# Twenty-two transfers move from SyncE's queue to GpSimd's in an attention and experts kernel

## The chip, the cores and the metric

The kernel runs on one core of a Trainium2 chip. The core has TensorE (PE), VectorE (DVE), ScalarE (ACT), GpSimd (POOL) and SyncE (SP). SP does no arithmetic here: it waits for semaphores and issues transfers. The metric is the device time of one execution in microseconds (us); lower is better. Times without another name are places in the one profiled execution, counted from its first instruction.

## The reference

A layer of cross attention is followed by a layer of nine experts, all in float32. `ctx` has 77 rows per batch, so each of 16 heads has 77 keys.

```python
# x (4, 1024, 256), ctx (4, 77, 256), fside (4, 16)
def xattn(x, latents, shift, scale, ...):
    xn = layernorm(x, ln1_w, ln1_b)          # x is ctx here
    ln = layernorm(latents, ln2_w, ln2_b)    # latents: the normalised input
    q = (ln @ Wq) * (1 + scale) + shift
    k, v = split(xn @ Wkv)
    attn = softmax(q @ k.T * DIM_HEAD ** -0.5)
    return (attn @ v) @ Wout
def ffn(x, Wr, Wg, Wu, Wd):
    probs = softmax(x @ Wr); two largest of nine, made to sum to one -> cw
    hidden = silu(x @ Wg[e]) * (x @ Wu[e])
    return sum over e of cw[e] * (hidden @ Wd[e])
x = x + xattn(ctx, norm(x), fside, fside, ...)
x = x + ffn(norm(x), ...)
```

## The kernel before

The 4096 tokens are cut into eight groups of 512 (`g`), and each group into four sub-blocks of 128 tokens. That makes 32 sub-blocks (`i`). After a preparation of the weights, the attention's loop runs over the sub-blocks. The experts follow: each takes blocks of 128 or 256 tokens that were routed to it.

**One turn of the attention's loop.** TensorE makes the scores of sub-block `i` (`scores`), ScalarE their exponentials (`exponentials`). VectorE makes the attention's weights of sub-block `i-1` in the tile `an` (`attention_weights`) and turns them in blocks of 32 into `anT`, of which there is one buffer. `weights_turn` has SyncE write `anT` to a scratch tensor in HBM (`a_d`, line 332) and, when that has landed, read it back in another order into `aT` (line 335, four transfers). Three sub-blocks later, `values` lets TensorE use `aT` as its stationary operand (`po`, line 344), and `attended` adds the product to the input in place, in the tile `x` of that group. Four buffers hold four groups' `x`.

**What is done once per group, at fixed turns of the loop.** For turn `i = 4g + s`:
- `load_x(g + 2)`, at `s = 1`: the input two groups ahead comes in, 512 KB, 4 KB in each of 128 partitions. Groups 0 and 1 are loaded ahead of the loop. Two turns later VectorE takes its statistics (`query_stats`, `bn_q`).
- `residual`, at `s = 3`, for group `g - 1`: the finished sum is written to the output (512 KB, line 861). The experts later add their part to the output there (`adding`, line 1378, indirect transfers on POOL).
- `places`, at `s = 3`, for group `g - 2`: eight indirect transfers on POOL write the group's entries into the experts' lists in HBM (`list_d`, line 965). Each moves 128 entries of 8 bytes.
- `normalised`, at `s = 0`, for group `g - 2`, counted from the turn it is in: ScalarE makes the experts' normalised input `y`, which is written to the scratch tensor `y_d` (512 KB, line 896). The experts gather their tokens from it (`inputs`, lines 1208 and 1225).
- `choices`, at `s = 1`: the routing. POOL makes three tiny tiles for it (lines 932 and 937).

**What sets the order.** The order on each engine is the order of the program's text. A transfer is issued when its engine's queue comes to it and its semaphores allow, and an instruction that waits holds everything behind it on that engine. On SyncE the order of one turn is: `a_d` of the last sub-block, the wait for it, its four `aT` reads, then what that turn has of the group's three transfers, then `a_d` of the next. From about 322 us on, the first experts' weights come in on SyncE too (lines 1191 to 1201).

Of the kernel before, what the change touches and what calls it, by code (L numbers as in the profile page):

```python
# [15 lines left out]
P = 128  # L16
# [5 lines left out]
def kernel(  # L22
# [18 lines left out]
    nc = tc.nc  # L41
# [11 lines left out]
    NS = TB // P  # L53
# [37 lines left out]
    x_v = x.flatten_outer_dims().rearrange("(g p s) d -> g p s d", p=P, s=NS)  # L91
    out_r = out.flatten_outer_dims()
    out_v = out_r.rearrange("(g p s) d -> g p s d", p=P, s=NS)
# [5 lines left out]
    y_d = dram.tile([TOK, D], F32, name="y_d")  # L99
# [102 lines left out]
    xg = {}  # L202

    def load_x(g):
        xg[g] = pools["xpool"].tile([P, NS, D], F32, tag="x", name=f"x{g}")
        nc.sync.dma_start(out=xg[g], in_=x_v[g])

    zscale, zstats = {}, {}

# [21 lines left out]
    def off_mean(name, g, mv, r):  # L231

        o = stat.tile([P, NS], F32, tag=name, name=f"{name}{g}")
        nc.vector.scalar_tensor_tensor(o, mv[:, :, 0], -1.0, r, ALU.mult, ALU.mult)
        return o
# [128 lines left out]
    with ExitStack() as kvs:  # L364
# [104 lines left out]
        for b in range(B):  # L469
# [12 lines left out]
            out=wrow, in_=ln2_w.rearrange("(o d) -> o d", o=1).to_broadcast([P, D])  # L482
# [105 lines left out]
        def router_weights():  # L588
# [26 lines left out]
            out=before, in_=ones, pattern=[[1, P]], compare_op=ALU.is_gt, fill=0.0, base=0,  # L615
# [64 lines left out]
        kvs.close()  # L680
        open_attention()
        load_x(0)
        load_x(1)
        for b in range(B):
            nc.vector.tensor_copy(g_sb[b][:, :, HJ:], wz)
            for t in range(2):
                for k in range(NP // QT):
                    nc.sync.dma_start(
                        out=g_sb[b][P - 1 : P, C - 1, :HJ].rearrange(
                            "p (q t k j) -> p q t k j", q=QT, t=2, j=J  # L690
                        )[:, :, t, k, :],
                        in_=brow.rearrange("(q r) k m -> q r k m", q=QT)[
                            :, t * B + b, k, b * J : (b + 1) * J
                        ],
# [163 lines left out]

    def residual(g):

        nc.sync.dma_start(out=out_v[g], in_=xg[g])
        mv = stat.tile([P, NS, 2], F32, tag="mvf", name=f"mv_f{g}", bufs=2)
        st = fstats.pop(g)
        for s in range(NS):
            yield nc.vector.bn_aggr(mv[:, s, :], st[:, s, :])
        routed[g] = dict(mv=mv)
# [19 lines left out]
    def normalised(g):  # L886

        y = pools["rpool"].tile([P, NS, D], F32, tag="y", name=f"y{g}", bufs=1)
        r = routed[g]["r"]
        o = off_mean("fo", g, routed[g]["mv"], r)  # L890
        for s in range(NS):
            yield nc.scalar.activation(
                y[:, s, :], xg[g][:, s, :], AF.Identity,
                bias=o[:, s : s + 1], scale=r[:, s : s + 1],
            )
        nc.sync.dma_start(out=y_d.rearrange("(g p s) d -> g p s d", p=P, s=NS)[g], in_=y)

    def choices(g):

# [540 lines left out]
    def routing(g):  # L1440

        yield from residual(g)
        root(g)
        yield from logits(g)
        exponential(g)
        yield from normalised(g)
        yield from choices(g)
        yield from listed(g)
# [9 lines left out]
    for i in range(N_SUB + 1):  # L1458
        g, s = divmod(i, NS)
        now_on = i < N_SUB  # L1460
        d = i - LAG
# [44 lines left out]
        if s == 1 and g + 2 < NG:  # L1506
            load_x(g + 2)
# [5 lines left out]
        if gr >= 0 and sr == 1:  # L1513
            if g + 2 < NG:
                query_variance(g + 2)
            if q >= 0:
                advance(residual(q))
                root(q)
            if g + 2 < NG:
                query_root(g + 2)  # L1520
            nc.scalar.activation(junk, eps_t, AF.Exp)
            if q > 0:
                advance(places(q - 1))
        if gr >= 0 and sr == 2 and q >= 0:
            advance(logits(q))
            exponential(q)
            advance(normalised(q))
# [125 lines left out]
```

## Time and profile before

| What | Value |
|---|---|
| median of 3 executions | 898.35 us (897.76 to 902.75) |
| the profiled execution's own time | 902.66 us |
| its span, first to last instruction | 900.6 us |
| TensorE busy in the span | 869.1 us, 97% |
| VectorE, ScalarE, GpSimd busy | 592.2, 356.2, 312.5 us |
| SyncE's transfers (q1 of the page) | 162.90 MB, 60.5% of 16 engines' time |
| GpSimd's transfers (q0) | 17.26 MB, 10.3% |
| granted TensorE clock, mean | 0.992 |

The profiled execution is one of its own: 902.66 us lies 4.31 us above the median. The span leaves 2.06 us of it outside. A row of waits says which instruction waited for what, for how long in total, how often, and at most. A row of the timeline has the start, the duration, the engine, the line, and in brackets the idle time of the engine just before it. In the windows, "DMA share" is the mean busy share of the core's 16 transfer engines, and GB/s is what they moved. [...]

### The profile page before, as it was taken

How to read it: one execution, taken by the hardware profiler on the slowest of the kernel's cores; microseconds unless marked ns; L12 is line 12 of the kernel's file. 1: busy time of each engine (PE TensorE's matmuls, PEld its weight loads, DVE VectorE, ACT ScalarE, POOL GpSimd, SP SyncE). 2: the span in 40 equal slices, each digit the busy share in tenths (PEclk: the TensorE clock that was granted, in tenths of full speed). 3: DMA queues.
4: the chain of work that ended last, by engine and by line, in shares of the span. 5: the costliest groups of instructions: out<-in, count | busy, mean ns of one | idle time of the engine just before them, and what ended most of it. 6: DMA issues, size and time to landing. Idle time of an engine off the chain costs nothing. (4 is left out here: it accounts for less than half of the span.)

```text
span 900.6 us, 13822 instructions
## 1 busy us (share of the span) xinstructions
PE 869.1 (97%) x3864; PEld 677.8 (75%) x3864; DVE 592.2 (66%) x1806; ACT 356.2 (40%) x1500; POOL 312.5 (35%) x325
## 2 busy tenths in 40 slices
PE   8999999998999998899999999999999999999996
PEld 6545787866787776788787777777777777778885
DVE  4857788778999978443826666666666656665641
ACT  3668687858788685241121111111111111111110
POOL 3000000404233430537256435435445435445232
PEclk9999999999999999899999999999999999999998
DMA  6116556566766676899579779779779778789722
GB/s 222 49 67 202 152 187 193 113 182 149 216 176 191 188 210 203 213 298 185 158 226 298 218 220 315 223 217 311 224 221 317 219 217 218 226 230 322 217 33 24
DMA packets 132956, 181.18 MB, mean 201 GB/s; under 512 B 26951, under 2 KB 98127, under 8 KB 132752
## 3 DMA queue, kind: packets, MB, share of 16 engines
q1 hardware_dynamic: 115322, 162.90, 60.5%
q0 software_dynamic: 17344, 17.26, 10.3%
q8 instruction: 31, 0.51, 0.3%
q14 instruction: 45, 0.37, 0.1%
q10 hardware_dynamic: 214, 0.13, 0.0%
HBM read 141.54 MB, written 40.39 MB: 202 GB/s over the span
## 5 line engine op out<-in xcount | busy, mean ns | idle before, releaser
L1265 PE MATMUL pg<-xT,wgu 128*128 128x256 f32 x1144 | 253.0, 380 | 3.0 <-DVEq L1606 1.5
L1265 PEld LDWEIGHTS pg<-xT,wgu 128*128 128x128 f32 x1144 | 215.5, 190 | 33.0 <-ACT xT L1254 2.5
L286 ACT ACTIVATE ex<-psc,mx 128x77 f32<-128x77 f32 x512 | 158.7, 331 | 70.3 <-DVE mx L275 66.6
L1343 PE MATMUL po<-wd,hid 128*128 128x256 f32 (+1 forms) x804 | 180.9, 380 | 0.0
L1343 PEld LDWEIGHTS po<-wd,hid 128*128 128x128 f32 (+1 forms) x804 | 149.2, 187 | 28.1 <-issue 3.7
L344 PE MATMUL po<-u,aT 128*128 128x265 f32 x640 | 159.2, 405 | 8.8 <-DMA aT<-a_d 8.8
L344 PEld LDWEIGHTS po<-u,aT 128*128 128x128 f32 x640 | 150.4, 313 | 11.6 <-issue 9.9
L1378 POOL DMA_INDIRECT out_dram<-co,ids x63 | 100.2, 1591 | 167.7 <-DVE co L1346 139.4
L965 POOL DMA_INDIRECT list_d<-r_entry,r_pli x64 | 66.8, 1043 | 260.9 <-DVE r_pli L963 148.1
L1238 DVE STREAM_TRANSPOSE xT<-yin 32x128 f32<-32x128 f32 (+1 forms) x544 | 148.4, 273 | 12.5 <-DMA yin<-y_d,ids 3.7
L271 PE MATMUL psc<-g,zT 128*128 128x462 f32 (+1 forms) x384 | 141.5, 514 | 2.6 <-ACT zT L260 2.6
L1271 ACT ACTIVATE sl<-pg 128x256 f32<-128x256 f32 x130 | 49.7, 384 | 233.8 <-PE pg L1265 162.1
L1272 DVE TENSOR_TENSOR hid<-pg,sl 128x256 f32<-128x256 f32 x130 | 55.0, 424 | 128.9 <-ACT sl L1271 94.7
L271 PEld LDWEIGHTS psc<-g,zT 128*128 128x128 f32 x384 | 71.7, 190 | 61.0 <-issue 46.0
L286 ACT ACTIVATION_READ_ACCUMULATOR ex<-psc,mx 128x1 f32 x512 | 107.9, 211 | 0.0
L327 DVE STREAM_TRANSPOSE anT<-an 128x1280 f32<-128x1280 f32 x32 | 79.6, 2486 | 14.3 <-DMA a_d<-anT 13.8
L1208 POOL DMA_INDIRECT yin<-y_d,ids x67 | 70.5, 1053 | 27.0 <-issue 25.5
L275 DVE TENSOR_REDUCE mx<-psc 128x6 f32<-128x462 f32 (+1 forms) x96 | 53.5, 558 | 18.8 <-PE psc L271 17.7
L1346 DVE TENSOR_SCALAR co<-po,ids 128x256 f32<-128x256 f32 x67 | 32.2, 483 | 48.4 <-PE po L1343 46.8
L308 DVE TENSOR_TENSOR an<-ex,rs 128x1024 f32<-128x1024 f32 x32 | 39.2, 1225 | 1.1
L1331 ACT COPY hid<-ph 128x384 f32<-128x384 f32 x15 | 7.2, 479 | 78.4 <-PE ph L1326 78.4
L1307 ACT ACTIVATE hs<-psg 128x512 f32<-128x512 f32 x15 | 9.0, 597 | 65.3 <-issue 42.2
(311 smaller groups left out, 762.5 us busy)
## 6 DMA issues: line engine op xcount, KB each, us to landing
wgu<-in_L_ffn_Wg_dram SPq DMA_DIRECT2D x41, 704.0 KB
wd<-in_L_ffn_Wd_dram SPq DMA_DIRECT2D x41, 640.0 KB
wgu<-in_L_ffn_Wu_dram SPq DMA_DIRECT2D x41, 512.0 KB
a_d<-anT SPq DMA_DIRECT2D x32, 640.0 KB
aT<-a_d SPq DMA_DIRECT2D x128, 160.0 KB
wgu<-in_L_ffn_Wu_dram SPq DMA_DIRECT2D x41, 128.0 KB
x<-in_x_dram SPq DMA_DIRECT2D x8, 512.0 KB
out_dram<-x SPq DMA_DIRECT2D x8, 512.0 KB
```

What stands on the lines that cost most here:

```text
L271: nc.tensor.matmul(psc[:, :w], zT[:, c, :], g_sb[i // NS // GPB][:, c, h * J : h * J + w], start=(c == 0), stop=(c == C - 1),)
L275: nc.vector.tensor_reduce(nmx[i][:, h : h + n], psc[:, : n * J].rearrange("p (h j) -> p h j", h=n), AX.X, ALU.max, negate=True,)
L286: nc.scalar.activation(exs[i][:, h + q, :], pscs[k][:, q * J : (q + 1) * J], AF.Exp, bias=nmx[i][:, h + q : h + q + 1], accum_out=sms[i][: ...
L327: nc.vector.transpose(turned.rearrange("p q t k -> p q k t"), an_of[0].rearrange("p (k q t) -> p q k t", q=NQ, t=Q))
L344: nc.tensor.matmul(po[:, :DE], aT[:, :, n], u_sb[b][:, n, :], start=(n == 0), stop=(n == KC - 1))
L965: i = nc.gpsimd.indirect_dma_start(out=list_d[:, :], out_offset=bass.IndirectOffsetOnAxis(ap=place_i[:, s : s + 1], axis=0), in_=entries[k ...
L1208: return nc.gpsimd.indirect_dma_start(out=dst, out_offset=None, in_=src, in_offset=bass.IndirectOffsetOnAxis(ap=offsets, axis=0), **kw,)
L1238: yield nc.vector.transpose(xT[q : q + Q].rearrange("p c (h t) -> p h c t", t=P)[:, :nh, :, a : a + Q], of(yins, j)[a : a + Q].rearrange(" ...
L1265: nc.tensor.matmul(pg[:, g, :], w[:, c, at : at + P], xT[:, c, :], start=(c == 0), stop=(c == C - 1),)
L1272: nc.vector.tensor_tensor(hid[:, f, :], pg[:, 1, :], sl, ALU.mult)
L1343: nc.tensor.matmul(po[rows, :D], hid[:, f, at], d[:, f, :], start=(f == 0), stop=(f == NF))
L1378: i = nc.gpsimd.indirect_dma_start(out=out_r, out_offset=bass.IndirectOffsetOnAxis(ap=rows_of(j, h, rows), axis=0), in_=cos[j][:, h, :], i ...
```

## The change

Three transfers of each group change the engine that issues them: the input from the third group on (6 transfers), the residual (8) and the experts' input (8). The computation, the tiles, the buffers and the place in the program's text are the same.

```diff
@@ load_x
-        nc.sync.dma_start(out=xg[g], in_=x_v[g])
+        (nc.sync if g < 2 else nc.gpsimd).dma_start(out=xg[g], in_=x_v[g])
@@ residual
-        nc.sync.dma_start(out=out_v[g], in_=xg[g])
+        nc.gpsimd.dma_start(out=out_v[g], in_=xg[g])
@@ normalised
-        nc.sync.dma_start(out=y_d.rearrange("(g p s) d -> g p s d", p=P, s=NS)[g], in_=y)
+        nc.gpsimd.dma_start(out=y_d.rearrange("(g p s) d -> g p s d", p=P, s=NS)[g], in_=y)
```

In the instruction lists of the two programs TensorE's, VectorE's and ScalarE's order is the same. SyncE's list loses the 22 transfers; the `a_d` writes and `aT` reads stay on it, beside the weights. On GpSimd's list they stand, for one group in the middle of the loop, as: residual of group `q`, the eight list entries of group `q-1`, experts' input of group `q`, input of group `q+4`, the three tiny tiles of the routing of `q`. The inputs of groups 2 and 3 stand at the head of this stretch, right behind the three clearing instructions (lines 198 and 200) that open the attention. The residual of the last group stands behind the eight list entries of group 6, with the last experts' input behind it, and then the first `adding`.

## The prediction, made before the changed kernel ran

> **What bounds the kernel.** The page's first part comes first: TensorE is busy 97% of the span, so a change can save only in its gaps, and can lose by making new ones. The moved transfers all lie between 34 and 404 us. I therefore asked who waits for whom, in the whole span (columns: total us, times, longest).
>
> ```profile
> PE po L344 <- DMA aT<-a_d: 8.8, 5, 3.6
> DVE anT L327 <- DMA a_d<-anT: 13.8, 7, 3.4
> SPq L335 <- DMA a_d<-anT: 144.7, 30, 9.9
> SPq L206 <- DVE num L639: 19.1, 1, 19.1
> DVE bn_q L213 <- DMA x<-in_x_dram: 2.1, 1, 2.1
> POOL list_d L965 <- DVE r_pli L963: 148.1, 3, 127.9
> ```
>
> The loop's own path to HBM and back is what reaches TensorE: `a_d` late stops VectorE (one `anT` buffer), `aT` late stops TensorE. SP's long waits are for `a_d` itself, not for the moved transfers. Next, SP's timeline shows what stands in front of a late `a_d`:
>
> ```profile
> 150.56 0.34 SPq L332 DMA_DIRECT2D a_d<-anT  x1
> 153.56 1.74 SPq L335 DMA_DIRECT2D aT<-a_d  x4
> ...
> 164.14 0.43 SPq L861 DMA_DIRECT2D out_dram<-x  x1
> 168.94 0.34 SPq L332 DMA_DIRECT2D a_d<-anT  x1
> 178.84 1.75 SPq L335 DMA_DIRECT2D aT<-a_d  x4
> 180.68 0.38 SPq L896 DMA_DIRECT2D y_d<-y  x1
> 181.37 0.34 SPq L332 DMA_DIRECT2D a_d<-anT  x1
> 189.43 1.74 SPq L335 DMA_DIRECT2D aT<-a_d  x4
> 191.22 0.43 SPq L206 DMA_DIRECT2D x<-in_x_dram  x1
> 191.99 0.34 SPq L332 DMA_DIRECT2D a_d<-anT  x1
> ```
>
> From `a_d` to its `aT` is its latency: 3.0 us with a free queue (150.56 to 153.56), 8.1 behind `y` (181.37 to 189.43), 7.9 behind `x` (191.99, its `aT` at 199.88), 9.9 behind the residual and beside eight list transfers (163.6 to 174.2). TensorE's timeline shows what arrives:
>
> ```profile
> 186.82 4.91 PE L344 MATMUL po<-u,aT 128*128 128x265 f32 x20 [2.08 <-DMA aT<-a_d]
> ...
> 207.97 0.44 PE L258 MATMUL pz<-ident,z 128*128 128x128 f32 x2 [2.38 <-ACT z L249]
> ...
> 358.69 6.56 PE L344 MATMUL po<-u,aT 128*128 128x265 f32 x20 [3.57 <-DMA aT<-a_d]
> ...
> 379.16 6.56 PE L344 MATMUL po<-u,aT 128*128 128x265 f32 x20 [2.31 <-DMA aT<-a_d]
> ```
>
> With gaps of 0.55, 0.21, 0.51 and 0.87 us (at 227, 232, 247, 308), the middle has 6.6 us of gaps, the end of the attention 6.2 with one of 0.32 at 350. The last two cost more than idle time: their twenty matmuls take 6.56 us instead of 4.86, because the granted clock is 0.50 at 360 to 362 and 0.54 at 382 to 384. Outside these, TensorE runs turn after turn of 9.1 us without a gap, and nothing can be won.
>
> **SP's sequencer.** It loses 14 issues of 0.43 and 8 of 0.38 us, 9.0 us in all. SP waits 144.7 us for `a_d` anyway: 0.
>
> **POOL's sequencer.** It gains 22 issues. The nearest rows are its two transfers with 128 rows, 0.57 and 0.56 us, with 0.30 us between issues: 22 x 0.87 = 19 us, in a stretch in which POOL is mostly idle (in 260 to 280 it does nothing). In order of the queue, the waits: a residual waits for VectorE's sum, done 10 us before the list entries behind it can start; `y` waits for ScalarE, which is done (172.9) before those entries (174.2); the input behind it needs the residual landed two turns earlier; the three tiny tiles then come at 176.5, and VectorE uses them at 193.7. Cost 0. Without that cover, list entries 2 us late would still be in time: the first gather of the lists is at 299.
>
> **The start.** Inputs 2 and 3 no longer wait for SP's turns (input 2 was issued at 75.0, input 3 at 110.0): they stand behind a memset at 34.7 to 35.0 and start beside inputs 0 and 1 (34.6). VectorE already waits 2.09 us there, until 38.41, and TensorE hangs on this by ScalarE's chain at 45.4. The windows show inputs 0 and 1 moving at 270 to 401 GB/s from 36 to 39. If POOL's data flows from 37 at an even share of 400, the 150 KB left of input 0 take 0.4 us longer. Input 1 lands near 41.3 instead of 39.8, and is wanted at 41.3. Bounds: 0, and 2.6 us (1 MB at 400 GB/s put fully in front). Taken **+0.4**.
>
> **The middle, what goes.** `a_d` no longer stands behind `y` and `x` in one queue. The gaps that hang on this are 2.38, 0.21, 0.51 and 0.87, 4.0 us. But the residual, free of SP's wait for `aT`, now goes when VectorE's sum is done (194.3 for group 2, before 208.4), which meets the `a_d` issued at 191.99. Bounds -4.0 and 0. The Trainium skill ("DMA: Bandwidth & Descriptors", section "Issuing engines are not separate DMA queues") says that transfers from several issuers run on the same 16 engines and interleave, so another issuer saves only issue time. By this rule the term is 0; by the row (8.1 and 7.9 against 3.0 us, for 512 KB that needs 1.3 us at 400 GB/s) it is -4.0. The row is about order rather than sharing, so I lean to it: **-2.5**. The residual is also gone from in front of the `a_d` at 168.94; its 9.9 us are mostly the list entries' (the window from 171 has a share of 1.67 at 58 GB/s), so of the gaps 2.08 and 0.55 I take **-1.0** (bounds -2.6 and 0).
>
> **The middle, what comes.** `y` and the next input now go right behind the list entries, at 174.3 and 175.3, no longer at 180.7 and 191.2. The late `aT` is issued at 178.84, and TensorE stands waiting for it at 184.7. Between them the engines are empty:
>
> ```profile
> 174.00:175.50 1.50, 1.50 (x8) 1.14 (x7) 1.50 (x3) 1.25 (x9) 1.02 (x4) 1.00 0.19 14
> 177.00:178.50 1.50, 1.50 (x9) 1.50 (x8) 0.00 (x0) 0.74 (x5) 0.00 (x0) 1.00 0.00 0
> ```
>
> The last two columns are the share and GB/s. 1 MB needs 2.6 us at 400 GB/s: if it flows there, it is hidden; if not, it lies in front of `aT`. Bounds 0 and 5.9 us (2.6 in groups 1 and 2, and in group 3, whose `aT` had some 1.9 us to spare, 0.7). Nearer to hidden, 0.5 each time: **+1.0**.
>
> **The end.** The residual of group 6 waits for a sum done at 348.8. It went at 361.66; it now goes near 349, beside the `a_d` of 346.63, whose `aT` TensorE awaits at 358.69. From 350.3 this `a_d` has about 450 KB left, so by bytes 1.1 us at 400 GB/s. The skill's page, section "Queues, rings and completion order", adds that a completion lands only after all earlier writes of that transfer engine, across its queues: then the whole 512 KB may count, 1.3 us at that rate. No row shows which; I take 1.1 by the windows (419 GB/s at 350, 161 at 351). In return the last `a_d` (363.41, 10.7 us) has 512 KB less in front, but `y` of group 6 (ScalarE done at 366.2, list entries at 368.9) goes at 369 instead of 375.9 and meets it: -0.4. Together **+0.7**. Bounds: -4.0 (the gap at 379.16 with its slow 1.7 us gone), +4.0 (both `aT` later by 512 KB, with more of the slow clock).
>
> **Behind it.** The last residual and `y` now go at 403 and 404 behind list entries. The first `adding` (407.31) needs the residual landed, 403.4 + 3 to 4 us, so up to 1 us late. POOL then has 15.0 us idle at 445 and no engine waits for it: 0. Without this cover, 1 us.
>
> **Sum.** 0.4 - 2.5 - 1.0 + 1.0 + 0.7 = -1.4: this execution's 902.66 would be 901.3. The median lies 4.3 below it, perhaps with shorter gaps, so I carry the difference, not the level: 898.35 - 1.4 = **897.0 us**.
>
> **Rivals.**
> - *The queue in front was all of it* (chance 0.20). Every gap of the middle goes, 6.6 us, the last gap with its slow clock half, 2.0; the start costs 0.4: 898.35 - 8.2 = 890.2. For it: 8.1 and 7.9 against 3.0. Against it: the same bytes still move, and the 9.9 us were beside list entries.
> - *The moved transfers overtake the late `aT`* (0.28), slower. Before, one queue kept `y` and `x` behind `aT`. Now, where the hole behind the list entries doesn't take them, they move with it: 2.6 + 2.6 + 0.7 in the middle, then 1.3 at 358 and 1.3 at 379, 8.5 us. It decides from the point at which `aT` is more than 2 us later than now. With the slow clock behind one gap more (1.7) and half of the middle's gains kept (-1.9) it gives 898.35 + 8.3 = 906.7. For it: `aT` is on the path at four places and the middle turns have no slack. Against it: the windows above are empty.
> - *POOL blocks* (0.04), slower: a residual or `y` that waits for a landed transfer holds the list entries and then the first gathers. It needs more than 20 us of delay at 299 to reach the experts at 365. Against it: every wait named above is over in time. A stall of 5 us at the first block would give 903.
>
> **The numbers.** My own case has 0.48; its range from the bounds, ends not all at once, is 893.5 to 902. The range for 8 in 10 reaches to the first rival's 890 and cuts the second's upper part: 890 to 905.5. About 0.5% (4.5 us) is what a measurement of this kernel can tell from no change. Faster by more is the first rival and 0.02 of my own case: 0.22. Slower by more is the other two, less a share of 0.04 that stays below 902.8, with 0.02 of my own: 0.30. The rest is 0.48.
>
> **What would show it.** Right: `a_d` near 3 to 4 us in two turns of each group, the gap at 208 gone, the waits of VectorE for `a_d` down from 13.8 us, `bn_q` at the start waiting 2.1 to 3 us. Wrong: `po` waiting longer than 8.8 us for `aT` in total (second rival); the 9.9 us down to 5 (first); POOL idle on ScalarE or on `out_dram` ahead of list entries (third).

## The result, and the profile after

The changed kernel takes 901.96 us (median of 20 executions, 897.04 to 905.43), the kernel before 898.06 us (20 executions, 893.27 to 904.1). The ratio is 1.0052, with a 95% interval of 1.0036 to 1.0067: the change costs about 4.7 us by the ratio (the two medians lie 3.9 us apart). The profiled execution took 903.41 us for a span of 901.5 us, at a mean granted clock of 0.986. The profiled execution of before was 902.66 us, an unusually long one for that kernel, so the two profiles lie only 0.8 us apart. Where the time goes is therefore read from pieces of the span, not from its end.

The page's parts on engines, queues and transfers (the last column of an issue is the median time from issue to landing, in us):

```profile
PE 871.0 (97%) x3864; PEld 679.4 (75%) x3864; DVE 591.6 (66%) x1806; ACT 355.9 (39%) x1500; POOL 323.9 (36%) x347
...
q1 hardware_dynamic: 112154, 151.37, 56.5%
q0 software_dynamic: 20512, 28.80, 15.7%
...
out_dram<-x POOLq DMA_DIRECT2D x8, 512.0 KB, 4.3
y_d<-y POOLq DMA_DIRECT2D x8, 512.0 KB, 6.4
```

The 22 transfers are now on q0: it has 11.5 MB more, and q1 11.5 MB less (22 x 512 KB). The change did what it says. TensorE's work is the same, yet it is busy 1.9 us longer: some of it ran at a lower clock, as shown below.

The view of waits of the changed kernel, in the whole span, SyncE's own ahead of it (columns: total us, times, longest):

```profile
SPq L335 <- DMA a_d<-anT: 149.5, 32, 13.7
...
ACT ex L286 <- DVE mx L275: 75.4, 68, 8.1
...
DVE anT L327 <- DMA a_d<-anT: 17.2, 8, 7.6
...
POOL out_dram L1378 <- DMA out_dram<-x: 9.4, 1, 9.4
PE po L344 <- DMA aT<-a_d: 9.3, 4, 3.7
...
PEld psc L271 <- ACT lg L297: 6.1, 3, 5.0
...
PE psc L271 <- DVE r_o L916: 4.3, 1, 4.3
...
DVE bn_q L213 <- DMA x<-in_x_dram: 2.2, 1, 2.2
```

The longest wait for an `a_d` rose from 9.9 to 13.7 us, VectorE's waits for it from 13.8 to 17.2, and a wait that before did not have stops TensorE: 4.3 us for scores. Its named releaser, `r_o`, is only the VectorE instruction that came last: nothing in the scores needs it. Two other lines of the view show the way. The scores' weight load (PEld) waits 5.0 us for `lg`, the last of ScalarE's readings of the previous scores, from the same PSUM buffer. ScalarE's exponentials wait 8.1 us for `mx` of VectorE, and `mx` stands on VectorE behind `anT`. What held VectorE there is in its own timeline:

```profile
181.59 2.43 DVE L327 STREAM_TRANSPOSE anT<-an 128x1280 f32<-128x1280 f32 x1 [7.62 <-DMA a_d<-anT]
```

VectorE stood 7.62 us because the one `anT` buffer was still being written to HBM. SyncE's and GpSimd's timelines of the changed kernel give the times around it:

```profile
167.43 0.34 SPq L332 DMA_DIRECT2D a_d<-anT  x1
181.56 1.73 SPq L335 DMA_DIRECT2D aT<-a_d  x4
184.05 0.34 SPq L332 DMA_DIRECT2D a_d<-anT  x1
191.56 1.73 SPq L335 DMA_DIRECT2D aT<-a_d  x4
194.08 0.34 SPq L332 DMA_DIRECT2D a_d<-anT  x1
```

```profile
171.65 0.97 POOL L965 DMA_INDIRECT list_d<-r_entry,r_pli  x1 [0.30 <-issue]
172.60 0.61 POOL L896 DMA_DIRECT2D y_d<-y  x1
173.19 0.60 POOL L206 DMA_DIRECT2D x<-in_x_dram  x1
```

The `a_d` issued at 167.43 lands by 181.56, after 14.1 us, where before it took 9.9. `y` and the next input were issued right behind the list entries, 8.4 us ahead of that landing. The windows of the same stretch (busy us and count of PE, PEld, DVE, ACT, POOL, then granted clock, DMA share, GB/s):

```profile
175.00:177.00 2.00, 2.00 (x11) 2.00 (x10) 0.00 (x0) 1.21 (x8) 0.00 (x0) 1.00 1.63 155
177.00:179.00 2.00, 2.00 (x9) 1.67 (x9) 0.00 (x0) 0.00 (x0) 0.00 (x0) 1.00 1.37 61
179.00:181.00 2.00, 2.00 (x6) 0.95 (x5) 0.00 (x0) 0.00 (x0) 0.00 (x0) 1.00 1.03 39
...
185.00:187.00 2.00, 1.13 (x2) 0.84 (x3) 1.70 (x9) 1.30 (x7) 0.00 (x0) 0.50 0.99 259
```

The engines that stood empty before from 177 to 178.5 now have a share of half to four fifths of these windows, but move 155, 61 and 39 GB/s, far from the 400 of the prediction. The share sums the time that packets took, and packets overlap: from 169 to 170 it is 2.68 in a window of 1 us. So it tells that packets are under way, and not how full an engine is. VectorE does nothing in the first three windows, and from 177 on ScalarE neither. The last row has the second price: the granted clock, which fell within TensorE's gap, is 0.50. TensorE's timeline shows all of it (brackets: idle time before the row):

```profile
185.87 2.48 PE L271 MATMUL psc<-g,zT 128*128 128x317 f32 x4 [4.29 <-DVE r_o L916]
...
190.06 6.78 PE L344 MATMUL po<-u,aT 128*128 128x265 f32 x20 [1.28 <-DMA aT<-a_d]
...
231.17 6.55 PE L344 MATMUL po<-u,aT 128*128 128x265 f32 x20 [2.22 <-DMA aT<-a_d]
...
362.50 7.56 PE L344 MATMUL po<-u,aT 128*128 128x265 f32 x20 [3.70 <-DMA aT<-a_d]
...
383.66 4.94 PE L344 MATMUL po<-u,aT 128*128 128x265 f32 x20 [2.09 <-DMA aT<-a_d]
```

Starts of the same TensorE instruction (us), changed kernel against before, add up the account:

| Instruction | before | after | difference |
|---|---|---|---|
| `pz`, first of the loop | 45.44 | 43.92 | -1.5 |
| `psc` ahead of the first late `a_d` | 161.73 | 160.20 | -1.5 |
| `psc` behind it | 191.57 | 196.67 | +5.1 |
| `psc` | 222.00 | 224.30 | +2.3 |
| `psc` behind the next one | 232.22 | 237.55 | +5.3 |
| `po` | 358.69 | 362.50 | +3.8 |
| first `po` of the experts | 399.04 | 401.92 | +2.9 |
| last `down` | 887.05 | 888.01 | +1.0 |

Between the second and the third row 6.6 us are lost: gaps of 4.29 + 1.28 in place of 2.08 (3.5), and at the slow clock `po` 6.78 for 4.91 us (1.9) and `psc` 2.48 for 1.3 (1.2). The gap at 208 goes and gives 2.8 us back, and the next group loses 3.0 again. Of the smaller gaps, 1.4 us go later. From the first row to the experts this makes 4.4 us (-1.5 to +2.9), close to the loss that the times show. The first row has nothing to do with the change. An instruction ahead of all moved transfers, the clearing of `z`, starts between 33.0 and 33.6 us in ten and between 34.7 and 35.3 in six of the sixteen profiles, of kernels with and without moved transfers. This before had a late start and this after an early one. The experts give 1.9 us back in these two executions; 1.3 of it is a gap at 437 of before that the changed one lacks, and whether the change has to do with it isn't shown.

### The profile page after: what moved, and what is told of

Read it like the earlier page. It is cut to its first block, busy times and chain, and to the rows that moved or that the text cites. A ratio compares the mean times of both kernels' runs of the same rounds, so it can differ in the third digit from the quotient of the medians.

```text
span 901.5 us, 13854 instructions
## 1 busy us (share of the span) xinstructions
PE 871.0 (97%) x3864; PEld 679.4 (75%) x3864; DVE 591.6 (66%) x1806; ACT 355.9 (39%) x1500; POOL 323.9 (36%) x347
## 5 line engine op out<-in xcount | busy, mean ns | idle before, releaser
L344 PE MATMUL po<-u,aT 128*128 128x265 f32 x640 | 162.1, 410 | 9.4 <-DMA aT<-a_d 9.3
L327 DVE STREAM_TRANSPOSE anT<-an 128x1280 f32<-128x1280 f32 x32 | 79.5, 2484 | 17.2 <-DMA a_d<-anT 17.2
L861 POOL DMA_DIRECT2D out_dram<-x x8 | 4.7, 587 | 152.8 <-DVE lg L353 152.8
```

Source lines behind the costliest of these rows:

```text
L327: nc.vector.transpose(turned.rearrange("p q t k -> p q k t"), an_of[0].rearrange("p (k q t) -> p q k t", q=NQ, t=Q))
L344: nc.tensor.matmul(po[:, :DE], aT[:, :, n], u_sb[b][:, n, :], start=(n == 0), stop=(n == KC - 1))
```

## The experiments

The theory after the result was that `y` and the next input overtake the late `a_d` and its `aT`. The rivals were the residual, GpSimd's kind of queue, the inputs of groups 2 and 3 at the start (theory C below), and the list entries alone. Each kernel was timed with the kernel before on the same chip. The chips differ (the median of before was 899.4, 895.76, 898.47 and 892.33 us in the four batches), so only the ratios are compared.

### One moved transfer at a time

Three kernels each keep one of the change's three lines, over the kernel before. A fourth keeps the lines of `y` and of the input:

```diff
@@ only y and the input moved
-        nc.sync.dma_start(out=xg[g], in_=x_v[g])
+        (nc.sync if g < 2 else nc.gpsimd).dma_start(out=xg[g], in_=x_v[g])
...
-        nc.sync.dma_start(out=y_d.rearrange("(g p s) d -> g p s d", p=P, s=NS)[g], in_=y)
+        nc.gpsimd.dma_start(out=y_d.rearrange("(g p s) d -> g p s d", p=P, s=NS)[g], in_=y)
```

> Only the residual's eight transfers go on GpSimd's queue; y and x stay on SyncE's, behind the turn's aT. Theory A (y and the next x, put right behind the list entries, share the transfer engines with the late a_d and aT): not slower, 893 to 899, a_d beside the list entries of group 1 still near 10 us. Theory B (any bulk transfer on GpSimd's queue costs the loop): slower by about a third of 4.7 us. Theory C (inputs 2 and 3 at the start): as before, 898.

> Only y's eight transfers go on GpSimd's queue. Theory A: slower by 1 to 4 us, the a_d beside the list entries of group 1 over 11 us. Theory B: a third, 1.6 us. Theory C: 898.

> Only the inputs from group 2 on go on GpSimd's queue; they stand there right behind the list entries. Theory A: slower by 1 to 4 us, the a_d beside the list entries of group 1 over 11 us. Theory B: 1.2 us. Theory C: all of the loss, 4.7 us, and bn_q at the start later.

> y and the inputs on GpSimd's queue, the residual on SyncE's. Theory A: all of the loss or more, 902 to 906. Theory B: two thirds, 901. Theory C: 4.7 us.

| Moved | median us | ratio (95%) | the late `a_d`, us | the next two, us |
|---|---|---|---|---|
| residual | 897.22 | 0.9983 (0.9964 to 1.0002) | 8.9 | 7.5, 7.3 |
| `y` | 899.62 | 1.0001 (0.9984 to 1.0018) | 10.9 | 4.1, 6.9 |
| input | 902.26 | 1.0015 (0.9989 to 1.0042) | 10.7 | 5.6, 3.8 |
| `y` and input | 905.89 | 1.0058 (1.0034 to 1.0082) | 11.4 | 7.3, 4.1 |

Alone, no line has a cost that the measurement can tell from none; the 1 to 4 us and the `a_d` of over 11 us that theory A expected of each did not come. `y` and the input together cost the whole loss, 5.2 us (0.0058 x 899.4), where the two alone add to 1.4, with wide intervals. The last two columns suggest why they don't add, from one profile of each kernel. Each one alone lengthens the late `a_d` by about 1 us against 9.9, but takes itself away from in front of a later one (8.1 and 7.9 before; 4.1 with `y` moved, 3.8 with the input moved). Together they both lie beside the late `a_d`, and the one after it then takes 7.3. The residual has no part in the loss that can be told. For the start: VectorE's wait there (`bn_q`) is 2.2 us with `y` and the input moved, 3.6 with the input alone, 2.1 before. The hold below has the same two inputs at the start and is faster than before, so the start doesn't make the loss.

### The same transfers from ScalarE's queue

```diff
@@ over the changed kernel
-        (nc.sync if g < 2 else nc.gpsimd).dma_start(out=xg[g], in_=x_v[g])
+        (nc.sync if g < 2 else nc.scalar).dma_start(out=xg[g], in_=x_v[g])
...
-        nc.gpsimd.dma_start(out=out_v[g], in_=xg[g])
+        nc.sync.dma_start(out=out_v[g], in_=xg[g])
...
-        nc.gpsimd.dma_start(out=y_d.rearrange("(g p s) d -> g p s d", p=P, s=NS)[g], in_=y)
+        nc.scalar.dma_start(out=y_d.rearrange("(g p s) d -> g p s d", p=P, s=NS)[g], in_=y)
```

> y and the inputs from group 2 on are issued by ScalarE instead of GpSimd, y right behind its four activations at the same time as in the changed kernel or 1 to 2 us sooner; the residual stays on SyncE's queue. Theory A: as slow as with y and x on GpSimd's queue, 902 to 907. Theory B': it is the kind of queue of GpSimd that costs: 896 to 900.

Measured: 901.78 us, 1.007 (1.0051 to 1.009). SyncE's timeline of this kernel:

```profile
169.31 0.34 SPq L332 DMA_DIRECT2D a_d<-anT  x1
180.79 3.33 SPq L335 DMA_DIRECT2D aT<-a_d  x4
```

The same late `a_d`, 11.5 us, with no moved transfer on GpSimd. So GpSimd's kind of queue is not needed for the loss. The timing is not quite that of the kernel with both on GpSimd: `y` went at 173.34, but the input stood on ScalarE behind exponentials that waited, and went at 183.67, among the `aT` reads, whose issue then took 3.33 us in place of about 1.74. What the two kernels share is that the transfers start without regard to SyncE's order.

### The list entries left out

In these two kernels the 64 transfers of list entries are not issued, so the lists keep the values that they are filled with, and the experts' gathers and additions skip rows. Their level of time is therefore not that of the whole kernel; they are read against each other and in the attention's loop.

```diff
@@ places, over the kernel before and over the changed one
-            for s in range(NS):
+            for s in range(0):
                 i = nc.gpsimd.indirect_dma_start(
```

> The kernel before without the 64 list entries' transfers: the lists stay at their filling, so that the experts' gathers and additions skip all rows; the rest of the work stays. Theory A: faster by the gaps of groups 1 and 2, 3 to 8 us, also by less work of the additions; a_d near 6 us at most in groups 1 to 4.

> The changed kernel without the 64 list entries' transfers, as in the run beside it. Theory A: the loss of 4.7 us is gone against that run (-2 to +1 us), since no a_d is late when y and x come. Theory B: the loss stays, 3 to 5 us.

Measured: 886.74 us, 0.9904 (0.9874 to 0.9934), without the change; 883.37 us, 0.9858 (0.9831 to 0.9885), with it. So without list entries the change's sign turns: it is then 3.4 us faster, a little beyond the -2 to +1 that was expected. SyncE's timeline of the first, with `y` still in its queue:

```profile
167.46 0.34 SPq L332 DMA_DIRECT2D a_d<-anT  x1
170.47 1.75 SPq L335 DMA_DIRECT2D aT<-a_d  x4
172.31 0.38 SPq L896 DMA_DIRECT2D y_d<-y  x1
176.44 0.34 SPq L332 DMA_DIRECT2D a_d<-anT  x1
179.42 2.41 SPq L335 DMA_DIRECT2D aT<-a_d  x4
```

From 160 to 300 us every `a_d` of this kernel takes 3.0 to 3.3 us (3.0 to 4.5 with the change), the one behind `y` too; `y` now has 4.1 us before the next `a_d` is issued. In the kernel before it had 0.7 (180.68 to 181.37), since the `aT` of that turn had come late. The list entries make the first `a_d` late, and a late turn makes `y` and the input collide with what follows. In the middle TensorE then has no gap that a transfer ends, in either kernel; the change's gain shows at the end of the attention, where a gap of 3.51 us at 348 with a slow `po` (6.37 us) becomes one of 0.64 without.

### Holding `y` and the input behind the turn's `aT`

Over the changed kernel, `y` and the next input keep GpSimd's queue, but wait until the `aT` reads of the turn have landed. If overtaking is the cause, this must take the loss away.

```diff
@@ weights_turn
-            nc.sync.dma_start(out=aT[q * Q : (q + 1) * Q], in_=by_key[q])
+            last_turned.append(nc.sync.dma_start(out=aT[q * Q : (q + 1) * Q], in_=by_key[q]))
+
+    def behind_turned(i):
+        for other in last_turned[-NQ:]:
+            tc.add_manual_dep(i.ins, other.ins.name, ...)
@@ load_x
+        if g > 3:
+            behind_turned(i)
@@ normalised
-        nc.gpsimd.dma_start(out=y_d..., in_=y)
+        behind_turned(nc.gpsimd.dma_start(out=y_d..., in_=y))
```

> The changed kernel, but on GpSimd's queue y and the next input wait until the aT reads of the turn have landed. Same queue, same bytes, same transfers. Theory A (overtaking of the late a_d and aT): the loss is gone, 895 to 900, no a_d over 11 us. Theory B (bulk transfers on GpSimd's queue as such): the loss stays, 902 to 905.

Measured: 890.88 us, 0.9953 (0.9936 to 0.9971): faster than the kernel before, and more so than the 895 to 900 us expected. GpSimd's timeline, and under it TensorE's, of this kernel:

```profile
171.45 0.97 POOL L976 DMA_INDIRECT list_d<-r_entry,r_pli  x1 [0.30 <-issue]
185.37 0.59 POOL L907 DMA_DIRECT2D y_d<-y  x1 [12.95 <-DMA aT<-a_d]
192.78 0.57 POOL L206 DMA_DIRECT2D x<-in_x_dram  x1 [6.82 <-DMA aT<-a_d]
```

```profile
184.80 4.94 PE L355 MATMUL po<-u,aT 128*128 128x265 f32 x20 [2.11 <-DMA aT<-a_d]
```

GpSimd now waits 12.95 us with `y`, with nothing urgent behind it. The late `a_d` takes 9.4 us and TensorE's gap is back at 2.11 us without a slow clock. The gap at 208 does not return. A window of the same kernel shows that the hole is empty again while that `a_d`, which lands by 176.64, is still under way:

```profile
175.00:177.00 2.00, 2.00 (x11) 2.00 (x10) 0.33 (x1) 1.05 (x7) 0.00 (x0) 1.00 0.00 0
```

Two variants tell what in the hold does it. One puts the residual back on SyncE; the other holds only until the turn's `a_d` has landed, and not its `aT` (here `last_turned` collects the `a_d` writes in place of the `aT` reads). A repeat of the changed kernel ran beside them on the same chip.

```diff
@@ first: residual, over the hold
-        nc.gpsimd.dma_start(out=out_v[g], in_=xg[g])
+        nc.sync.dma_start(out=out_v[g], in_=xg[g])
@@ second: behind_turned, over the hold
-        for other in last_turned[-NQ:]:
+        for other in last_turned[-1:]:
```

> y and the next input held on GpSimd's queue until the turn's aT has landed; the residual back on SyncE's queue. If the held version's gain over the kernel before is the hold's: 892 to 895. If it is the residual's (alone 0.9983): near the kernel before, 897 to 899.

> All three on GpSimd's queue; y and the next input wait until the turn's a_d has landed, not its aT. If they overtake a_d: as good as the full hold, 890 to 895. If they overtake aT: as slow as the changed kernel, 900 to 904. In between if both.

> The changed kernel again, on the chip of the two runs beside it: slower than the kernel before by 0.3 to 0.8%, the a_d beside group 1's list entries 11 us or more.

Measured: residual back 888.1 us, 0.9959 (0.9935 to 0.9982); held for `a_d` alone 891.39 us, 0.9995 (0.9978 to 1.0011); the changed kernel again 894.26 us, 1.0023 (1.0005 to 1.004). So the gain is the hold's, and the residual adds nothing to it that can be told. With the hold for `a_d` alone, `y` was issued at 176.17, as the `aT` reads began, and the late `a_d` took 8.5 us; but six gaps of TensorE (0.4 to 2.1 us) stayed, against two with the residual back and the full hold. Its ratio lies between the two others, which suggests that `aT` is overtaken too; its interval overlaps both of theirs, so the size of this share is open. The repeat of the changed kernel lost 0.23%, less than the 0.3 to 0.8% expected, with a late `a_d` of 12.3 us and gaps of 2.46 and 1.90, against 0.52% in the first comparison, with 14.1 us and 4.29 and 1.28. Whether that is the chip or the scatter isn't shown; the two intervals overlap.

### The list entries in two lots

If eight list transfers at once make the `a_d` late, four at once and four a turn later could make it less so.

```diff
@@ the loop, over before, the changed kernel and the hold
-                advance(places(q - 1))
+                placing = places(q - 1)
+                advance(placing, 5)
         if gr >= 0 and sr == 2 and q >= 0:
+            if q > 0:
+                advance(placing)
             advance(logits(q))
```

> The kernel before, with each group's eight list entries' transfers in two lots of four, the second lot and its two VectorE instructions one turn later. If eight in a row make a_d late (theory A's first half): a_d beside them 5 to 7 us, no gap at 186 or 208, 890 to 896. If it is their number in the whole loop: no change, 898.

> The changed kernel with the list entries in two lots of four. Here y and the next input stand behind the second lot. Theory A: the a_d of that turn is the one that is late, by less than with eight in a row; less loss than the changed kernel against its own partner (the run beside it), 0 to 3 us instead of 4.7. Theory B: 4 to 5 us.

> y and the next input held until the turn's aT has landed, with the list entries in two lots of four. If both add up: 885 to 890, faster than holding alone (890.9, ratio 0.9953). If the late a_d was only dear because y and x came on top: as holding alone.

Measured: over the kernel before 898.53 us, 1.0003 (0.9985 to 1.002); over the changed one 904.19 us, 1.0077 (1.0051 to 1.0103); over the hold 896.2 us, 0.9978 (0.9959 to 0.9997). A miss: the longest `a_d` of that group takes 8.7 us (9.9 undivided), 10.5 (14.1) and 10.4 (9.4). The lots shorten it in two of three kernels, each read from one profile, and no time is won by it.

## Why the prediction was wrong, step by step

The prediction forecast -1.4 us and gave no change the best chance; the kernel became 4.7 us slower. The second rival, "The moved transfers overtake the late `aT`", came closest, and its sign came, if barely: `po` waits 9.3 us for `aT`, against 8.8. But what the transfers held up first was the `a_d`, and the larger gap reached TensorE by VectorE and the scores. Of the signs for the forecast, two came (an `a_d` of 3 to 4 us in two turns of a group, the gap at 208 gone) and one failed (VectorE's waits rose). The forecast's range, 890 to 905.5, holds the time.

- **"The middle, what comes" (+1.0): the step that failed.** It took the empty engines between 174 and 178.5 for free room. The room was not free. The `a_d` of that time was still under way, and the transfers that were put into it moved at 155 to 39 GB/s, while that `a_d` took 14.1 us in place of 9.9. Leaving the same transfers out of the hole turns a loss into a gain (the hold, 0.9953). The step also priced a late `aT` only. A late `a_d` stops VectorE as well, by the one `anT` buffer, and through it the scores: 4.29 us. And it put the slow clock at nothing, which was 3.1 of the first late turn's 6.6 us. Its upper bound was 5.9 us for three groups; the first late turn alone cost 6.6 us and the next 3.0.
- **"The middle, what goes" (-2.5): right in sign, and too small.** The gap at 208 went, 2.8 us, and smaller ones, 1.4: 4.2 in place of 2.5. Each alone, `y` out of the queue brought the 8.1 us to 4.1, and the input out brought the 7.9 to 3.8. But these rows were the consequence of a late turn (3.0 us behind the same `y` where the turn was on time), and with both moved the `a_d` that took 8.1 still took 7.5. The rule of the Trainium skill that it weighed ("DMA: Bandwidth & Descriptors", "Issuing engines are not separate DMA queues") gave a term of 0, which the 4.2 us don't fit. The runs agree with it in that the issuer's kind doesn't matter (ScalarE's queue: 1.007). They show beyond it that one issuer's order was worth something, because it kept two transfers behind a chain that TensorE waits for (the hold puts them back behind it, 0.9953).
- **The residual (-1.0 in the middle).** Alone it gave 0.9983, -1.5 us with an interval of -3.2 to +0.2: it agrees, and can't be told from none. In the changed kernel the two gaps that it was to shorten grew, with `y` and the input beside them (2.08 to 4.29 and 1.28, 0.55 to 2.22).
- **The start (+0.4).** `bn_q` waits 2.2 us against 2.1: 0.1.
- **The sequencers (0).** A moved transfer takes GpSimd 0.53 to 0.62 us to issue, as the row said; no engine waited for it. GpSimd did not block, so the third rival is out.
- **The end (+0.7).** From 358.69 to 399.04 before, 362.50 to 401.92 after: 0.9 us shorter. The first gap is 0.1 longer and its `po` 1.0 slower (7.56 us); the second gap is 0.2 shorter and lost its slow clock (4.94 for 6.56). The first part was forecast at +1.1 and came at 1.1, but by a longer stretch of slow clock and not by a later `aT`: that is luck. The second was forecast at -0.4 and came at -1.8, nearly all of it slow clock.
- **"Behind it" (0).** The first `adding` waited 9.4 us for the residual, where the step said up to 1: the last residual was issued at 405.88, behind eight list entries. The cover that it named, GpSimd's later idle time, held: no TensorE gap follows.

What stays open: why an `a_d` of 640 KB, which alone lands in 3.0 us, is under way for 8 to 10 us beside list entries, while the profile shows no packet for the last of these. Leaving the entries out shows that they are the cause. It is not their load. Of GpSimd's queue from 160 to 190 us (packets, MB, share of the engines' time), the first line is the kernel before, which has only list entries there; the second is the changed kernel, and the third the changed kernel without list entries:

```profile
q0 software_dynamic: 256, 0.01, 0.6%
q0 software_dynamic: 544, 1.06, 40.6%
q0 software_dynamic: 288, 1.05, 9.3%
```

The entries' own packets take 0.6%. But the same `y` and input, 1.05 MB, take 9.3% without entries and some 40% with them. From issue to landing the changed kernel's view of that stretch has 11.0 us for an entry (median), 13.2 for `y` and 14.5 for the input; without entries `y` takes 4.9. So what moves beside the entries is slow to land, and the entries are too (9.6 us in the hold). The mechanism isn't shown, and splitting them did not help.

## What to carry to other kernels

Empty transfer engines are free room only if no transfer that an engine waits for is under way in that stretch; ask first what is about to land there. One queue's order can be what protects a chain of transfers that an engine waits for: when others are taken out of that queue, give them an explicit wait behind the chain. A row that shows a transfer held up in a queue may itself be the result of an earlier late one, so look for the first late transfer of the stretch before counting the gain of the rest.

## What the runs showed of the hardware

- Eight indirect transfers of 128 entries of 8 bytes stretch a 640 KB write to HBM beside them from 3.0 us to 8 to 10, with 0.00 share and 0 GB/s at the end of it (177 to 178.5, before). Their own packets take 0.6% of the engines' time (160 to 190, before): they don't keep the engines busy.
- Bulk transfers that start behind such entries move slowly too: 39 to 155 GB/s from 175 to 181, at a share of 50 to 80%. The 512 KB of `y` take 13.2 us to land, against 4.9 without entries.
- Gaps of nearly one length can slow TensorE's clock or not: 2.22 us at 231 (changed kernel), 2.31 at 379 (before) and even 1.88 at 350 (the hold) are followed by 6.55 to 6.57 us for a `po`; 2.38 at 208 (before) and 2.09 at 384 (changed kernel) are not (4.85 and 4.94).
- The issue of a transfer of 128 rows of 4 KB takes 0.33 to 0.36 us on ScalarE (its own run), 0.34 to 0.44 on SyncE (before) and 0.53 to 0.62 on GpSimd (changed kernel).
